# Transposing half of a group's attention probabilities with VectorE and a round trip through DRAM, in eleven of sixteen token tiles

## The chip, the core and the metric

The kernel runs on one core of a Trainium2 chip. The metric is the device time of one execution in microseconds (us). Engines are named as in the profile: PE (TensorE), PEld (its weight loads), DVE (VectorE), ACT (ScalarE), POOL (GpSimd), SP (SyncE, which here only issues DMAs).

## The reference

A transformer block in float32 on 4 sequences of 512 tokens, width 1024, 32 query heads and 8 key heads of 32 columns each:

```python
x = x + layernorm(attention(layernorm(x), w_qkv, b_qkv, w_o, b_o))
x = x + layernorm(lora_moe(layernorm(x), gate_w, base_w, base_b, lora_A, lora_B))

# attention
qkv = x @ w_qkv.T + b_qkv              # then rope on q and k
scores = einsum('bhqd,bhkd->bhqk', q, k) / sqrt(32), causal
attn = softmax(scores)
out = einsum('bhqk,bhkd->bhqd', attn, v) @ w_o.T + b_o
# lora_moe: a dense product x @ base_w.T, plus the two best of 8 rank-16 adapters
```

## The kernel before

The 2048 tokens are 16 tiles of 128 (four per sequence, i = 0 to 3 within it); a list `line` holds them in the order of the work, 0 to 11, 13, 14, 15, 12. Tiles go in pairs through the three big products (q, o and f): `seven` (L655) does a pair with seven products instead of eight, with sums of operands and of weights. Weight pieces of 128x512 (256 KB) come from DRAM into a ring of RING = 13 buffers, each for one product, in the order in which PE uses them (`bring_pieces`, L476). Keys, values and gate use weights that stay in SBUF.

**Attention of a tile** goes in groups (`Group`, L1371). A group has n heads of each of four key heads ("quads" r = 0 to 3), so that a quad's scores fill at most 512 columns: n = 4 for i = 0, 2 for i = 1, 1 for i = 2 and 3. It has m = n(i+1) blocks of 128x128 per quad. There are 88 groups. The steps of one group:

1. `scores` (L1382): PE writes q times k of the four quads, side by side on 32-row tiles of the array, into the one PSUM tile `sc`.
2. Softmax: DVE adds the mask and finds the negated maximum (two quads at a time, L1459 and L1469); ACT takes the exponentials with their sums into `pr` in SBUF (L1411); DVE inverts the sums (L1440); POOL scales `pr` (L1425).
3. `turn` (L1480), once per quad: PE transposes the m blocks of `pr` into PSUM (`pt_p`, L1485); `copy` brings them to SBUF as `prT`.
4. `values` (L1498): PE multiplies `prT` of the four quads, side by side, with v into `av` (L1508), and a copy brings that to `aT`, the input of product o.

`copy` (L331) may go to ACT (L335) or DVE (L336), whichever is free first. It serves `prT`, `aT`, and the turned x, h, k and low-rank tiles.

**What sets the order.** Every engine executes its instructions in the order in which they were issued; waits are semaphores. The order is worked out when the program is built, by a planner (`Order`, L92): operations have costs in us, are put on the engine where they start first, and PE picks the next step from lanes: scores, turns, the value lane (a group's four turns, then its values), and the dense products. `_choice` (L202) prefers what is ready; scores and values that could go together are put directly one behind the other, since both use tiled parts of the array:

```python
        value = values[0] if values and values[0].tiled else None
        waiting = []
        if score is not None and value is not None:
            if self._comes(score):
                waiting.append(values)
            if self._comes(value) and not self._is_ready(value):
                waiting.append(scores)
```

The value lane is filled at L1623: `value_lane += g.turned + [g.valued]`. A group's scores also wait for the turns of the group two before (L1611). `pr` and `prT` of one quad take one 2 KB slot each of SOFT = 8. PSUM has 4 banks (`ps`) besides `sc`. All DMAs are issued by SP, in order; an issue waits there for its buffer, and what stands behind it waits too. The planner counts 2.8 us from the end of a DMA's transfer until it has landed (LANDS) and 370 KB per us (RATE).

Of the kernel before, what the change touches and what calls it, by code (L numbers as in the profile page):

```python
# [11 lines left out]
F32 = mybir.dt.float32  # L12
# [4 lines left out]
P = 128  # L17
# [5 lines left out]
MASKED = -1e30  # L23
QUADS = P // HD


# [4 lines left out]
FILL = 0.3  # L31
# [60 lines left out]
class Order:  # L92
# [109 lines left out]
    def _choice(self, scores, values, lanes):  # L202
# [7 lines left out]
        if score is not None and value is not None:  # L210
            if self._comes(score):
                waiting.append(values)
            if self._comes(value) and not self._is_ready(value):
                waiting.append(scores)
        for lane in lanes:
# [20 lines left out]
    def tensor(self, scores, urgent, values, dense):  # L236


        while True:
# [17 lines left out]
            for step in steps:  # L257
                self._take(step)
            self.now += us
            for step in steps:  # L260
                step.done.finish(self.now + FILL)
        self.run(float("inf"))
# [3 lines left out]
def kernel(  # L266
# [26 lines left out]
    QSCALE = 1.0 / math.sqrt(HD)  # L293
    BANKS, SOFT, RING = 4, 8, 13

# [35 lines left out]
    def copy(n, out, in_):  # L331

        return Op(
            0,
            act=(0.15 + n * 0.00085, lambda: nc.scalar.copy(out(), in_())),  # L335
            dve=(0.15 + n * 0.00105, lambda: nc.vector.tensor_copy(out(), in_())),  # L336
        )
# [507 lines left out]
    for n, tok in enumerate(line):  # L845
        tok.before = line[n - 1] if n else None
        tok.last = n == T - 1
    pairs = [line[n : n + 2] for n in range(0, T, 2)]

    def load_x(job):  # L850
# [520 lines left out]
    class Group:  # L1371
        def __init__(self, tok, at, n):
            self.tok, self.seq, self.at, self.n = tok, tok.seq, at, n
            self.kt = at // GROUP
            self.name = f"{tok.t}_{at}"
            self.parts = 2
            self.exps, self.normed = [Task() for _ in range(QUADS)], [Task() for _ in range(QUADS)]
            self.rtot = [Task() for _ in range(QUADS // 2)]
            self.pr, self.prT = [None] * QUADS, [None] * QUADS
            self.has_prT = [Task() for _ in range(QUADS)]  # L1380

    def scores(g):  # L1382
# [19 lines left out]
        def quadrant(r):  # L1402
            urgent = 1 + r / QUADS
            yield soft_slots.take()
            pr = soft.tile([P, GROUP, P], F32, tag="soft", name=f"pr_{g.name}_{r}")
            pr = g.pr[r] = pr.rearrange("p a b -> p (a b)")
            for c in range(g.n):
                yield act(
                    0.5 + n * 0.00079,
                    urgent,  # L1410
                    lambda: nc.scalar.activation(  # L1411
                        pr[:, c * n : (c + 1) * n],
                        sc4[:, r, c, :],
                        AF.Exp,
                        bias=nmax[:, r, c : c + 1],
                        accum_out=total[:, r, c : c + 1],
                    ),
                )
            g.exps[r].finish(order.at)
            yield g.rtot[r // 2]  # L1420
            for c in range(g.n):
                yield pool(
                    0.33 + n * 0.00089,
                    urgent,
                    lambda: nc.gpsimd.tensor_scalar(  # L1425
                        pr[:, c * n : (c + 1) * n],
                        pr[:, c * n : (c + 1) * n],
                        rtot[:, r, c : c + 1],
                        1.0,
                        ALU.mult,  # L1430
                        ALU.mult,
                    ),
                )
# [10 lines left out]
        def softmax():  # L1444
# [8 lines left out]
            for r0 in range(0, QUADS, q):  # L1453
# [19 lines left out]
                for r in range(r0, r0 + q):  # L1473
                    start(quadrant(r), order.at)

        start(softmax(), order.now)
        for h in range(QUADS // 2):
            start(totals(h), order.now)

    def turn(g, r):  # L1480

        m = g.n * (g.tok.i + 1)
        pt = ps.tile([P, 4, P], F32, tag="ps", name=f"pt_p_{g.name}_{r}")
        for j in range(m):
            nc.tensor.transpose(pt[:, j, :], g.pr[r][:, j * P : (j + 1) * P], ident)  # L1485

        def end():
            yield g.turned[r].done
            soft_slots.give(order.at)
            yield soft_slots.take()  # L1490
            prT = g.prT[r] = soft.tile([P, NQ, P], F32, tag="soft", name=f"prT_{g.name}_{r}")
            yield copy(m * P, lambda: prT[:, :m, :], lambda: pt[:, :m, :])
# [5 lines left out]
    def values(g):  # L1498

        tok, i = g.tok, g.tok.i  # L1500
        if tok.aT is None:
            tok.aT = acts.tile([P, ND, P], F32, tag="aT", bufs=3, name=f"aT_{tok.t}")
        av = ps.tile([P, GROUP, P], F32, tag="ps", name=f"av_{g.name}")
        for c in range(g.n):
            for j in range(i + 1):
                for r in range(QUADS):
# [3 lines left out]
                        lhsT=g.seq.v[j][:, head * HD : (head + 1) * HD],  # L1510
                        rhs=g.prT[r][:, c * (i + 1) + j, :],
                        start=(j == 0),
# [3 lines left out]
        def end():  # L1516
            yield g.valued.done
            for r in range(QUADS):
                soft_slots.give(order.at)
# [86 lines left out]
    for k, g in enumerate(groups):  # L1606
# [4 lines left out]
        if k > 1:  # L1611
# [4 lines left out]
            Step(0.109 * blocks, partial(turn, g, r), [g.normed[r | 1]], bank=True, turns=True)  # L1616
            for r in range(QUADS)
        ]
# [3 lines left out]
        score_lane.append(g.scored)  # L1622
        value_lane += g.turned + [g.valued]  # L1623

# [129 lines left out]
```

## Time and profile before

| | |
|---|---|
| three runs, us | 1163.79, 1162.33, 1164.63; median 1163.79 |
| the profiled execution, us | 1164.45, its span 1162.7 |
| granted PE clock | 0.996 |
| instructions in the span | 21371 |
| HBM read, written | 209.09 MB, 20.97 MB: 198 GB/s over the span |
| pieces issued | 664 of 256 KB |
| pt_p transposes | 1280 (320 for each of the four quads) |

The span is the time between the first and the last instruction of the profile; the execution's time has 1.75 us around it. Busy times of an engine overlap with those of others, so they do not add up. A PE matmul's duration is longer than its spacing to the next one, since matmuls are pipelined; what PE spends is read from where the next one begins. One float32 product is two instructions, a transpose one. In the groups of the profile, "out<-in" names the tiles, x the count, then come busy us, mean ns of one, and the idle time before them with what ended it.

### The profile page before, as it was taken

Reading aid. Unit: us, or ns where it says so; the run is one execution under the profiler, and the core shown is the slowest. Engines: PE = TensorE matmul, PEld = TensorE weight load, DVE = VectorE, ACT = ScalarE, POOL = GpSimd, SP = SyncE. Lnnn points to the kernel's source line nnn. Section 1 sums busy time; section 2 is a strip of 40 time slices with the busy share of each in tenths; the row PEclk is TensorE's granted clock in tenths of the full one; section 3 lists DMA queues with packets and bytes.
Section 4 is the critical chain, followed back from the end, with each engine's and each line's share of the span. In section 5 each row is a group of like instructions: output and inputs, shape, how many; then the busy total and the mean of one; then the engine's idle time right before and its main releaser. Section 6 shows DMA issues by size and latency. Waiting matters only on the chain.

```text
span 1162.7 us, 21371 instructions
## 1 busy us (share of the span) xinstructions
PE 1136.4 (98%) x7240; PEld 624.5 (54%) x7240; DVE 832.6 (72%) x1629; ACT 530.1 (46%) x1545; POOL 611.7 (53%) x859
## 2 busy tenths in 40 slices
PE   7999999999999999999999999999999999999997
PEld 3455554655556455565555555456555555556443
DVE  4787767987678756787667876768866787668564
ACT  0354554555555355555434434455644555454010
POOL 2686856743756435544555253654545564547231
PEclk9999999999999999999999999999999999999999
DMA  9879777563773637625477443673457745585783
GB/s 349 277 255 310 248 253 263 170 220 97 257 239 96 199 109 253 192 83 176 141 244 256 137 135 118 219 229 106 149 168 233 243 135 160 164 268 187 221 285 118
DMA packets 117740, 231.48 MB, mean 199 GB/s; under 512 B 13440, under 2 KB 14464, under 8 KB 117632
## 3 DMA queue, kind: packets, MB, share of 16 engines
q1 hardware_dynamic: 117632, 230.12, 60.7%
q8 instruction: 58, 0.95, 0.3%
q14 instruction: 50, 0.41, 0.1%
HBM read 209.09 MB, written 20.97 MB: 198 GB/s over the span
## 4 chain that ended last, share of the span: by engine, by line
PE 86%; DVE 7%; DMA 3%; POOL 1%; ACT 1%; issue 1%; SPq 0%; POOLq 0%; ACTq 0%
PE acc_f L618 18%; PE acc_o L618 16%; PE acc_q L618 14%; PE pt_p L1485 11%; PE acc_kv L618 8%; PE sc L1390 7%; PE av L1508 6%; PE acc_gl L618 2%; DVE nmax L1469 2%; PE pt_xn L593 1%; PE pt_h L593 1%; DMA piece<-in_w_qkv_dram 1%; ACT pr L1411 1%; PE pt_q L1010 1%; DMA xa<-in_x_dram 1%
## 5 line engine op out<-in xcount | busy, mean ns | idle before, releaser
L1425 POOL TENSOR_SCALAR pr<-pr,rtot 128x256 f32<-128x256 f32 (+3 forms) x512 | 300.5, 602 | 251.9 <-DVE rtot L1440 183.3
L1411 ACT ACTIVATE pr<-sc,nmax 128x256 f32<-128x256 f32 (+3 forms) x512 | 265.0, 536 | 121.8 <-DVE nmax L1469 63.6
L1469 DVE TENSOR_REDUCE nmax<-sc 128x2 f32<-128x768 f32 (+3 forms) x176 | 198.2, 1126 | 33.7 <-ACT pr L1411 30.6
L1485 PEld LDWEIGHTS pt_p<-ident,pr 128*128 128x128 f32 x1280 | 144.5, 141 | 59.3 <-issue 49.1
L1485 PE MATMUL pt_p<-ident,pr 128*128 128x128 f32 x1280 | 173.2, 276 | 2.4 <-DVE raw_q L727 1.0
L335 ACT COPY prT<-pt_p 128x512 f32<-128x512 f32 (+1 forms) x261 | 134.1, 548 | 62.4 <-PE pt_p L1485 61.0
L1459 DVE TENSOR_TENSOR sc<-sc,cmask 128x256 f32<-128x256 f32 (+2 forms) x176 | 96.7, 550 | 48.6 <-PE sc L1390 39.0
L335 ACT COPY aT<-av 128x128 f32<-128x128 f32 (+2 forms) x83 | 26.1, 315 | 222.1 <-PE av L1508 222.0
L618 PE MATMUL acc_f<-piece,s_f 128*128 128x512 f32 x256 | 120.1, 602 | 2.1 <-DVE s_f L343 2.1
L618 PE MATMUL acc_kv<-wkv_sb,T_xn 128*128 128x512 f32 x256 | 119.4, 597 | 0.0
L1411 ACT ACTIVATION_READ_ACCUMULATOR pr<-sc,nmax 128x1 f32 x512 | 108.3, 212 | 0.0
L618 PE MATMUL acc_o<-piece,aT 128*128 128x512 f32 x232 | 105.9, 594 | 0.0
L618 PE MATMUL acc_q<-piece,s_q 128*128 128x512 f32 x224 | 105.4, 595 | 0.1
L618 PE MATMUL acc_q<-piece,T_xn 128*128 128x512 f32 x224 | 103.9, 594 | 0.1
L618 PE MATMUL acc_o<-piece,s_o 128*128 128x512 f32 x224 | 102.8, 593 | 0.0
L1390 PE MATMUL sc<-kT,qT 32*128 32x384 f32 (+3 forms) x1024 | 93.9, 464 | 0.5 <-ACT pr L1411 0.5
L1508 PEld LDWEIGHTS av<-prT,v 128*32 128x32 f32 x2560 | 64.8, 109 | 50.1 <-issue 35.0
L618 PE MATMUL acc_f<-piece,T_h 128*128 128x512 f32 x192 | 90.0, 592 | 0.0
L343 POOL TENSOR_TENSOR y<-y,w 128x512 f32<-128x512 f32 x61 | 79.1, 1309 | 20.3 <-ACT w L568 14.9
L1508 PE MATMUL av<-prT,v 128*32 128x128 f32 x2560 | 88.7, 276 | 0.2 <-DVE prT L336 0.2
L336 DVE COPY prT<-pt_p 128x512 f32<-128x512 f32 (+1 forms) x91 | 58.3, 642 | 31.3 <-PE pt_p L1485 29.7
L541 POOL TENSOR_TENSOR rstd<-veps,neg_half 128x1 f32<-128x1 f32 x64 | 35.0, 549 | 86.1 <-DVE veps L537 85.8
(154 smaller groups left out, 1416.3 us busy)
## 6 DMA issues: line engine op xcount, KB each, us to landing
piece<-mixed_f SPq DMA_DIRECT2D x128, 256.0 KB, 3.5
piece<-in_w_o_dram SPq DMA_DIRECT2D x116, 256.0 KB, 3.6
piece<-mixed_q SPq DMA_DIRECT2D x112, 256.0 KB, 3.4
piece<-mixed_o SPq DMA_DIRECT2D x112, 256.0 KB, 4.1
piece<-in_w_qkv_dram SPq DMA_DIRECT2D x100, 256.0 KB, 3.7
piece<-in_w_base_dram SPq DMA_DIRECT2D x96, 256.0 KB, 3.3
xa<-in_x_dram SPq DMA_DIRECT2D x32, 256.0 KB, 3.8
y<-in_x_dram SPq DMA_DIRECT2D x16, 512.0 KB, 5.7
```

The source lines that it names most:

```text
L335: act=(0.15 + n * 0.00085, lambda: nc.scalar.copy(out(), in_())),
L336: dve=(0.15 + n * 0.00105, lambda: nc.vector.tensor_copy(out(), in_())),
L343: engine.tensor_tensor(out=out(), in0=in0(), in1=in1(), op=op)
L541: nc.gpsimd.tensor_tensor(out=self.rstd, in0=self.veps, in1=neg_half, op=ALU.pow)
L618: nc.tensor.matmul(acc[0][:, :n], lhsT=lhsT(c), rhs=w(c), start=(c == 0), stop=last)
L1390: nc.tensor.matmul(sc[:, r, c * n : (c + 1) * n], lhsT=tok.qT[g.kt][rows, (g.at + c) % GROUP, :], rhs=seq.kT[g.kt][rows, :n], start=True, ...
L1411: lambda: nc.scalar.activation(pr[:, c * n : (c + 1) * n], sc4[:, r, c, :], AF.Exp, bias=nmax[:, r, c : c + 1], accum_out=total[:, r, c : ...
L1425: lambda: nc.gpsimd.tensor_scalar(pr[:, c * n : (c + 1) * n], pr[:, c * n : (c + 1) * n], rtot[:, r, c : c + 1], 1.0, ALU.mult, ALU.mult,),
L1459: lambda: nc.vector.tensor_tensor(out=diag, in0=diag, in1=cmask.unsqueeze(1).unsqueeze(1).to_broadcast([P, q, g.n, P]), op=ALU.add,),
L1469: lambda: nc.vector.tensor_reduce(nmax[:, some, : g.n], sc4[:, some], AX.X, ALU.max, negate=True),
L1485: nc.tensor.transpose(pt[:, j, :], g.pr[r][:, j * P : (j + 1) * P], ident)
L1508: nc.tensor.matmul(av[r * HD : (r + 1) * HD, c, :], lhsT=g.seq.v[j][:, head * HD : (head + 1) * HD], rhs=g.prT[r][:, c * (i + 1) + j, :], ...
```

## The change

In the eleven tiles `line[3:14]` (3 to 11, 13 and 14), quads 2 and 3 of every group are no longer turned by PE. There are 64 such groups: 24 with four blocks per quad of tiles with i = 3, 4 of i = 0 and 12 of i = 1 (also four blocks), and 24 of i = 2 with three blocks. For them:

- `pr` of a pair of quads is one tile, and for quads 2 and 3 its columns are laid out as (strip s of 32 keys, quad, block, key in strip), so ACT and POOL write runs of 32 floats.
- `flip`: DVE transposes the 32x32 blocks in place (one instruction of 128 x 2m·128), SP writes the tile to DRAM (`there`), waits until it has landed, and reads it back with four DMAs, one for each strip of keys, into `flat`, in runs of 2m·32 floats.
- `values` reads its moving operand for those quads as four strips of 32 columns.

Everywhere: a group's values stand behind the next group's turns in the value lane; `pr` and `prT` are kept by pairs of quads (SOFT = 6 slots of 4 KB instead of 8 of 2 KB); RING goes from 13 to 9; `copy` goes to ACT alone; `_choice` no longer holds scores back for values; and the planner takes the scores of a scores-and-values pair as done before the values.

```diff
-            if self._comes(value) and not self._is_ready(value):
-                waiting.append(scores)
...
+            first = self.now + (us if len(steps) == 1 else steps[0].us + TILING / 2)
             self.now += us
-            for step in steps:
-                step.done.finish(self.now + FILL)
+            for step, at in zip(steps, (first, self.now)):
+                step.done.finish(at + FILL)
...
-    BANKS, SOFT, RING = 4, 8, 13
+    BANKS, SOFT, RING = 4, 6, 9
+    FROM, TO = 3, 14
+    SIDE = 32
+    NS = P // SIDE
...
             act=(0.15 + n * 0.00085, lambda: nc.scalar.copy(out(), in_())),
-            dve=(0.15 + n * 0.00105, lambda: nc.vector.tensor_copy(out(), in_())),
...
+    flipped = line[FROM:TO]
...
+            self.by_tensor = QUADS // 2 if tok in flipped else QUADS
...
+            if r < g.by_tensor:
+                pr = g.pr[r // 2][:, r % 2]
+                to = [pr[:, c * n : (c + 1) * n] for c in range(g.n)]
+                exp_in = [sc4[:, r, c, :] for c in range(g.n)]
+                exp_out = to
+            else:
+                j = tok.i + 1
+                strips = g.pr[r // 2][:, :, r % 2]
+                to = [strips[:, :, c * j : (c + 1) * j, :] for c in range(g.n)]
+                exp_in = [
+                    sc4[:, r, c, :].rearrange("p (j s k) -> p j s k", s=NS, k=SIDE)
+                    for c in range(g.n)
+                ]
+                exp_out = [a.rearrange("p s j k -> p j s k") for a in to]
...
+    def flip(g):
+        m = g.n * (g.tok.i + 1)
+        h = g.by_tensor // 2
+        yield g.normed[g.by_tensor :]
+        pr = g.pr[h].rearrange("p s r m k -> p (s r m k)")
+        yield dve(
+            0.1 + 2 * m * P * 0.00105,
+            1,
+            lambda: nc.vector.transpose(out=pr, in_=pr),
+        )
+        there = dram.tile(
+            [NS, SIDE, NS, 2 * m * SIDE], F32, tag="there", bufs=4, name=f"there_{g.name}"
+        )
+        yield sp(
+            P * 2 * m * P * 4 / 1024 / RATE,
+            lambda: nc.sync.dma_start(out=there.rearrange("a k s r -> (a k) (s r)"), in_=pr),
+            -1,
+        )
+        yield LANDS
+        soft_slots.give(order.at)
+        yield soft_slots.take()
+        flat = g.prT[h] = g.new("flat", h)
+        def read():
+            for s in range(NS):
+                nc.sync.dma_start(
+                    out=flat[s * SIDE : (s + 1) * SIDE].rearrange("p a r m q -> p a (r m q)"),
+                    in_=there[:, :, s, :].rearrange("a k r -> k a r"),
+                )
+        yield sp(NS * 0.37, read, -1)
+        yield LANDS
+        for r in range(g.by_tensor, QUADS):
+            g.has_prT[r].finish(order.at)
...
+        def rhs(r, m):
+            prT = g.prT[r // 2]
+            if r < g.by_tensor:
+                return prT[:, r % 2, m * P : (m + 1) * P]
+            return prT[:, :, r % 2, m, :]
...
-                        rhs=g.prT[r][:, c * (i + 1) + j, :],
+                        rhs=rhs(r, c * (i + 1) + j),
...
-            for r in range(QUADS)
+            for r in range(g.by_tensor)
...
-        value_lane += g.turned + [g.valued]
+        value_lane += g.turned + ([groups[k - 1].valued] if k else [])
+    value_lane.append(groups[-1].valued)
```

In the issue order of the changed program SP has 64 writes to `there` and 256 reads of `flat` more.

## The prediction

> **What bounds the kernel now.** I read the busy table first, then the chain of work that ended last, then the groups, the waits and the DMA issues.
>
> ```profile
> PE 1136.4 (98%) x7240; PEld 624.5 (54%) x7240; DVE 832.6 (72%) x1629; ACT 530.1 (46%) x1545; POOL 611.7 (53%) x859
> ...
> PE 86%; DVE 7%; DMA 3%; POOL 1%; ACT 1%; issue 1%; SPq 0%; POOLq 0%; ACTq 0%
> ...
> L1485 PE MATMUL pt_p<-ident,pr 128*128 128x128 f32 x1280 | 173.2, 276 | 2.4 <-DVE raw_q L727 1.0
> L335 ACT COPY prT<-pt_p 128x512 f32<-128x512 f32 (+1 forms) x261 | 134.1, 548 | 62.4 <-PE pt_p L1485 61.0
> ...
> L336 DVE COPY prT<-pt_p 128x512 f32<-128x512 f32 (+1 forms) x91 | 58.3, 642 | 31.3 <-PE pt_p L1485 29.7
> ...
> q1 hardware_dynamic: 117632, 230.12, 60.7%
> ```
>
> PE is busy for 98% of the span and 86% of the chain is PE; the DMA queues' packets fill 60.7% of 16 engines. A PE instruction that goes away shortens the end, if nothing else holds PE up. The 276 ns on the transposes (the turns) is a latency, since matmuls overlap; the spacing comes from the chain in order of time (start, length, what):
>
> ```profile
> 92.24 1.31 PE pt_p L1485 x12
> ...
> 304.16 10.30 PE acc_o L618 x24
> ```
>
> A turn occupies PE for 1.31/12 = 0.109 us, and a 512-wide product (two instructions) for 2 x 10.30/24 = 0.858 us. In the timeline a group's scores of 512 columns take 1.07 us (750.68 to 751.75), its values 1.01 us (756.24 to 757.25). PE is idle for only 1162.7 - 1136.4 = 26 us, most of it at both ends, so time can come only from PE's own work.
>
> **What is removed.** In the issue order of the changed program PE has 816 pt_p transposes instead of 1280; all other PE counts are equal. 464 x 0.109 = **50.6 us off PE**. The 128 copies of those turns go (40 quad pairs of 512 columns, 24 of 384). All remaining PSUM copies are on ACT. By the rows (587 ns for 512 columns, 482 for 384, 266 to 372 for smaller ones), ACT's copies go from 183.7 to 202.4 us, so ACT stands at about 549 us of busy time; DVE loses 91.1 us of copies. A copy can now stand behind an exponential (0.69 + 0.21 us) where DVE used to take it. At the 58 copies of x, h, k and the low-rank tile that went to DVE, that is at most 52 us; at best nothing. I take nothing, since PE's waits for copies were 0.7 us (turns on ACT's prT) and 0.2 (values on DVE's): dense products lie between, and they stay.
>
> **What is added.** Sixty-four DVE block transposes, 40 of 128x1024 and 24 of 128x768. No such row exists. The nearest are DVE's reductions over the same sizes, 1223 and 957 ns: 40 x 1.223 + 24 x 0.957 = 71.9 us. DVE ends at 832.6 - 91.1 + 71.9 = 813 us, still under PE. Half price would be 36 us less, double 72 us more, which is 885 us and still hidden as busy time; only its 1 to 2.4 us in each group's own path counts.
>
> DMA: 464 blocks of 64 KB are 30.4 MB written and 30.4 MB read. 292 MB over some 1130 us is 258 GB/s. These 10 us stretches show what the queues carried:
>
> ```profile
> 10.00:20.00 10.00, 10.00 (x24) 4.45 (x23) 3.98 (x11) 0.00 (x0) 1.37 (x2) 1.00 1.07 378
> 20.00:30.00 10.00, 9.93 (x31) 4.63 (x30) 4.79 (x9) 0.59 (x1) 4.07 (x5) 1.00 1.05 393
> ```
>
> (The last column is GB/s.) So the mean fits; peaks may not.
>
> SP: 64 writes and 256 reads, 320 x 0.33 to 0.38 us = 106 to 122 us of issue on a queue that mostly waits for free piece buffers:
>
> ```profile
> SPq L489 <- PE acc_q L618: 231.7, 167, 20.6
> SPq L489 <- PE acc_f L618: 224.2, 184, 10.9
> ```
>
> Strided access: the softmax of the moved quads writes runs of 32 floats, and PE reads the values' moving operand in such runs. For POOL there is a row: the rotary product with a 32-wide broadcast (L780) takes 1321 ns, the plain addition of equal size 1309, so I count nothing. For ACT and PE none exists. DVE's 16-wide runs (565 ns for 256 elements, against 429 for the mask addition of 256) are a third dearer; on ACT that would be some 0.2 us per exponential, hidden by an engine idle half the time. For the values the bounds are nothing and double time, 232 blocks x 0.218 = 50.6 us (a group of four blocks takes 1.01, of which about 0.14 is the entry). I take nothing, since turns and products run at one column rate whatever the operand (0.109 for 128 columns, 0.429 for 512), and keep the upper end.
>
> Order: the before order has 74 values directly after scores, the changed one 57. The timeline shows about 0.09 us at entering tiled work (products of 3.44 us fill 3.53 before the scores at 763.44). 17 x 0.09 = **1.5 us**.
>
> **The new wait: values for the round trip.** A moved group's values wait for scores, softmax, block transpose, write, landing, four reads, landing. Behind the values on PE everything waits, since its order is fixed. From the timeline, scores' end to the last normalised quad takes (medians) 10.0 us for tiles of three key blocks, 10.8 for four, 13.8 for two, 18.9 for one. To this comes T: DVE 1.2, plus 0.4 for its queue; the write; four read issues, 1.3; the last landing. DMA landings:
>
> ```profile
> DMA to landing us min/median/max: 2.6/5.8/8.8
> ```
>
> is for the 512 KB stores of mixed weights. The 256 KB loads of x:
>
> ```profile
> DMA to landing us min/median/max: 2.7/3.8/6.6
> ```
>
> Middle: 1.6 + 5.8 + 1.3 + 3.8 = 12.5. Ends: 1.6 + 2.6 + 1.3 + 2.7 = 8.2 and 1.6 + 8.8 + 1.3 + 6.6 = 18.3.
>
> Against this stands the PE work that the order puts between a group's scores and its values. Laid end to end at the spacings above it is 21.6 to 38 us in tiles of three and four blocks (half of them under 26.5), 25.5 and more for two, 30.9 and more for one. Walking the 64 groups, each shortfall pushing all that follows, the stalls sum to: T = 11: 0; 12: 2; 13: 7; 14: 15; 16: 39; 18: 70 us. T = 12.5 gives 4; landings scatter, so I take **6 us**.
>
> **Fewer piece buffers, 13 to 9.** Along the orders, the PE work between the release of a buffer and the use of its next piece is at least 10.3 us before and 6.9 after; 85 of 655 have under 8. Piece landings are 3.1 to 4.3 us. But SP stands at a read until its write has landed: typically four pieces lie between, 3.4 us of PE work, against 5.8 for the landing. That is 2.4 us of waiting and 1.3 of issuing with pieces behind it, so the next piece is some 2.8 us late and needs 2.8 + 4 = 6.8, or 7.8 with a 5 us landing. Ends: nothing, and 1 us at half of the 64 groups, 32 us. I take **10 us**, a third of a microsecond at half of them.
>
> **Sum**, against the profiled execution's 1164.45 us (span 1162.7; the median of the runs is 1163.79, 0.1% lower): 1164.45 - 50.6 + 1.5 + 6 + 10 = **1131 us**.
>
> The Trainium skill speaks against the route. "VectorE: DVE Perf Modes", in "The three transpose paths", warns that a plain DMA copy with strides for a transpose is 19 times slower than the hardware's own when the innermost destination stride is large. No row of before shows such a copy; here DVE turns the 32x32 blocks and the reads keep runs of 768 or 1024 bytes, so the condition isn't met. If it held all the same, 30.4 MB at a nineteenth of 378 GB/s would alone take some 1500 us, an estimate by that page. "DMA: Bandwidth & Descriptors", "Anatomy of one DMA", gives about 2.0 us plus bytes over 436 GB/s on its other path: an estimate of 3.2 us for each way, T about 8, no late values and 1125 us. The trace's 5.8 us stores are dearer, and I go by them.
>
> **Rivals.**
> 1. *All is hidden.* For: the order leaves 21.6 us and more. Against: before's stores under load. 1164.45 - 50.6 + 1.5 = 1115.
> 2. *Pieces starve.* Nine buffers and a third more DMA traffic, above all in stretches of seven-product work with groups between, where about 7 pieces and 1 MB of round trip fall in some 8.7 us: 2.9 MB, 330 GB/s. For: landings there would be nearer to the first 160 us (6.0 us for pieces of w_qkv). Against: 378 GB/s was carried. The upper end, 32 us, with the 6: about 1153.
> 3. *The round trip is too long: slower.* Place: the values' wait for the four reads. If T is 16 or more, by small packets of 1 KB or by SP standing behind a piece, stalls of 39 us and 10 for pieces eat the 49; at T = 17 (54 us) with 10 it is 1179. The turning point is T = 16. For: the largest landings, 8.8 and 6.6. Against: medians stay at 12.5.
> 4. *The strided operand makes values dearer.* At the upper end 50.6 us: the gain is gone and with the 16 of stalls it ends at 1182; at half of that, 1156.
>
> **Chances.** Forecast (1116 to 1145) 0.45; all hidden 0.10; pieces 0.19, of which 0.02 within 0.2%; round trip 0.18; strips 0.08, of which 0.03 faster, 0.02 same, 0.03 slower. Faster by over 0.2% (what a measurement of this kernel can tell): 0.45 + 0.10 + 0.17 + 0.03 = 0.75; within: 0.04; slower: 0.21. The range 1110 to 1172 leaves out the dearest part of rivals 3 and 4, under 0.2. The forecast's sign holds most of the chance.
>
> **What would show it.** Right: 816 transposes at the same spacing; values waiting for the flat reads for under 10 us in all; PE 97% busy or more; DVE transposes near 1.2 us; stores landing in 5 to 6 us, reads in about 4. Wrong: LDWEIGHTS of the values waiting on a DMA for tens of us (rival 3); products waiting for pieces for over 20 us (rival 2); values of 1.01 us growing to 1.5 or more (rival 4). A DVE transpose of over 2.5 us, or exponentials a third dearer, would also break the sum, since every group's path lengthens with them.

## The result and the profile after

The changed kernel takes 1193.56 us (median of four runs, 1193.10 to 1194.06), the kernel before beside it 1163.13 (four runs): a ratio of 1.026, 95% interval 1.0242 to 1.0278. The change makes the kernel 30 us slower; 1131 us was forecast, and the range ended at 1172. The profiled execution took 1193.11 us, its span 1191.4, at a mean granted PE clock of 0.984 (before 0.996).

The page of the changed kernel, in its own order: busy times, the main DMA queue, the chain by engine, three groups, the issues of the round trip.

```profile
PE 1111.7 (93%) x6776; PEld 582.7 (49%) x6776; DVE 807.9 (68%) x1533; ACT 535.5 (45%) x1573; POOL 616.2 (52%) x863
...
q1 hardware_dynamic: 163712, 290.95, 76.8%
...
PE 47%; DMA 17%; DVE 3%; SPq 2%; POOL 1%; ACT 1%; issue 1%; POOLq 0%; ACTq 0%; DVEq 0%
...
L339 ACT COPY prT<-pt_p 128x512 f32<-128x512 f32 (+1 forms) x224 | 111.7, 552 | 64.6 <-PE pt_p L1566 53.8
L621 PE MATMUL acc_o<-piece,s_o 128*128 128x512 f32 x224 | 108.8, 616 | 22.6 <-DMA piece<-in_w_o_dram 14.1
...
L1566 PE MATMUL pt_p<-ident,pr 128*128 128x128 f32 x816 | 115.5, 281 | 9.3 <-DVE raw_q L730 4.2
...
there<-pr SPq DMA_DIRECT2D x40, 512.0 KB, 4.7
flat<-there SPq DMA_DIRECT2D x160, 128.0 KB, 4.6
```

The 464 turns are gone (x816), yet PE is idle for 1191.4 - 1111.7 = 79.7 us, 53 more than before, and DMA holds 17% of the span in the chain where it held 3% (the chain could be followed over 72% of the span only). The turns that are left keep their spacing (in the chains, where the clock is full, 16 of them take 1.76 to 1.90 us before and 1.90 after), so 464 x 0.109 = 50.6 us of PE's work were gained. The span grew by 28.7 us all the same: some 79 us were lost elsewhere, 53 of them as idle time of PE. The waits of PE and of its weight loads (us in total, times, longest), then those of SP's queue:

```profile
PEld acc_o L621 <- DMA piece<-in_w_o_dram: 20.3, 10, 4.4
PE acc_o L621 <- DMA piece<-in_w_o_dram: 14.1, 10, 3.5
PE av L1602 <- DMA flat<-there: 10.5, 7, 4.2
```

```profile
SPq L492 <- PE acc_q L621: 123.9, 103, 12.4
SPq L492 <- PE acc_f L621: 116.2, 143, 16.9
SPq L1549 <- DMA there<-pr: 103.4, 59, 5.3
```

All products together wait 23.8 us on PE for pieces, the values 10.5 for `flat`; in the kernel before PE has neither wait (only its weight loads wait for pieces, 15.5 us, here 45.7). SP stands at 59 reads until their store has landed, 103 us in all. One such place in the timeline (start, length, engine, line; in brackets the idle time before, with what ended it):

```profile
254.82 0.36 SPq L1539 DMA_DIRECT2D there<-pr  x1
255.30 1.29 SPq L872 DMA_DIRECT2D xa<-in_x_dram  x2
...
261.89 0.41 PE L1602 MATMUL av<-prT,v 128*32 128x128 f32 x4
261.93 1.75 SPq L1549 DMA_DIRECT2D flat<-there  x4
...
266.47 0.43 PE L1602 MATMUL av<-flat,v 128*32 128x128 f32 x2 [4.17 <-DMA flat<-there]
...
266.66 0.46 PE L1602 MATMUL av<-flat,v 128*32 128x128 f32 x2
...
266.87 0.46 PE L1602 MATMUL av<-flat,v 128*32 128x128 f32 x2
```

The store is issued at 254.82, the reads only 7.1 us later, the values run at 266.47: 11.65 us from the store's issue, and PE stands for 4.17. Then look at the last rows: the entries come every 0.21 us, where other values come every 0.11. The table of 2 us stretches says why (busy us of PE, PEld, DVE, ACT, POOL, each with its count; then the granted clock, the DMA share, GB/s):

```profile
262.00:264.00 2.00, 0.30 (x4) 0.03 (x3) 1.94 (x2) 0.77 (x3) 1.84 (x3) 1.00 0.42 125
264.00:266.00 2.00, 0.00 (x0) 0.00 (x0) 1.96 (x4) 0.68 (x3) 2.00 (x2) 0.87 0.98 290
266.00:268.00 2.00, 1.53 (x28) 1.50 (x28) 0.29 (x1) 0.00 (x0) 2.00 (x3) 0.50 0.94 383
268.00:270.00 2.00, 2.00 (x9) 1.25 (x6) 0.00 (x0) 0.79 (x3) 0.06 (x1) 0.50 0.81 169
270.00:272.00 2.00, 2.00 (x4) 0.88 (x3) 1.23 (x3) 0.74 (x3) 0.96 (x2) 0.50 0.83 280
272.00:274.00 2.00, 2.00 (x13) 0.70 (x12) 0.39 (x2) 0.59 (x1) 0.83 (x1) 0.92 0.23 84
```

After some 4 us without work the granted clock is 0.50 for 6 us. By an estimate from these rows, a stall of 4 us thus costs about 3 us more, in which PE is "busy". The Trainium skill, "TensorE: Matmul & The Clock Gate", Part 1, says the same: half the clock after an idle window of about 3.4 us, full clock after a busy one. Not every stall of that length shows it here: after one of 3.53 us, which ends at 629.13, the next two stretches of 2 us are at 1.00, and 0.53 comes only behind a further stall of 2.20 us.

A second place shows a stall of another kind, right behind a short wait for `flat`:

```profile
319.63 0.39 PE L1602 MATMUL av<-flat,v 128*32 128x128 f32 x4
...
320.06 0.59 ACT L339 COPY aT<-av 128x512 f32<-128x512 f32 x1 [2.03 <-PE av L1602]
...
324.89 0.66 DVE L346 TENSOR_TENSOR s_o<-s_o,aT 128x512 f32<-128x512 f32 x1
...
325.69 2.04 PE L621 MATMUL acc_o<-piece,s_o 128*128 128x512 f32 x2 [5.68 <-ACT pr L1442]
```

These values (1.3 us late) are the last of their pair. Product o needs their `aT` and its sum `s_o`, which DVE executes only at 324.89, behind masks and maxima of the next groups, which themselves wait for exponentials on ACT. PE has no other work in its order there, so it stands for 5.68 us more. (The releaser named, an exponential, isn't what the product reads; `s_o` is.) It is tempting to put this stall down to the late values, but it isn't theirs: in **a_values** and **a_tiny** below no value waits for the round trip on PE, and the stall is there all the same, 5.65 us long. It belongs to the order in which the planner put the work. Two more are like it: 4.16 us before the turns at 980.17 and 5.27 us before those at 1078.16. a_tiny has all three:

```profile
314.60 5.46 PE L621 MATMUL acc_o<-piece,s_o 128*128 128x512 f32 x6 [5.65 <-ACT pr L1442]
...
931.57 1.09 PE L1571 MATMUL pt_p<-ident,pr 128*128 128x128 f32 x4 [4.24 <-DVE raw_q L730]
...
1030.20 2.12 PE L596 MATMUL pt_h<-ident,w 128*128 128x128 f32 x8 [5.27 <-DVE w L565]
```

They are 15.1 of the changed kernel's 79.7 us of idle time. After its start the kernel before has no stall longer than 2.1 us.

### The profile page after: what moved, and what is told of

Same layout as the page of the kernel before. It is cut to its first block, busy times and chain, and to the rows that moved or that the text cites. A ratio compares the mean times of both kernels' runs of the same rounds, so it can differ in the third digit from the quotient of the medians.

```text
span 1191.4 us, 20840 instructions
## 1 busy us (share of the span) xinstructions
PE 1111.7 (93%) x6776; PEld 582.7 (49%) x6776; DVE 807.9 (68%) x1533; ACT 535.5 (45%) x1573; POOL 616.2 (52%) x863
## 3 DMA queue, kind: packets, MB, share of 16 engines
q1 hardware_dynamic: 163712, 290.95, 76.8%
## 4 chain that ended last, share of the span: by engine, by line
PE 47%; DMA 17%; DVE 3%; SPq 2%; POOL 1%; ACT 1%; issue 1%; POOLq 0%; ACTq 0%; DVEq 0%
PE acc_f L621 13%; PE acc_o L621 8%; PE acc_q L621 6%; DMA there<-pr 5%; DMA flat<-there 4%; PE sc L1408 4%; PE acc_kv L621 4%; PE pt_p L1566 4%; PE av L1602 3%; PE acc_gl L621 2%; DMA piece<-in_w_o_dram 1%; DMA out_dram<-y 1%; DMA piece<-mixed_q 1%; SPq L1549 1%; DVE nmax L1500 1%
## 5 line engine op out<-in xcount | busy, mean ns | idle before, releaser
L1490 DVE TENSOR_TENSOR sc<-sc,cmask 128x256 f32<-128x256 f32 (+2 forms) x176 | 97.1, 551 | 68.9 <-PE sc L1408 61.8
L339 ACT COPY prT<-pt_p 128x512 f32<-128x512 f32 (+1 forms) x224 | 111.7, 552 | 64.6 <-PE pt_p L1566 53.8
L621 PE MATMUL acc_o<-piece,s_o 128*128 128x512 f32 x224 | 108.8, 616 | 22.6 <-DMA piece<-in_w_o_dram 14.1
L1566 PE MATMUL pt_p<-ident,pr 128*128 128x128 f32 x816 | 115.5, 281 | 9.3 <-DVE raw_q L730 4.2
L621 PE MATMUL acc_kv<-wkv_sb,T_xn 128*128 128x512 f32 x256 | 122.6, 613 | 0.0
L1566 PEld LDWEIGHTS pt_p<-ident,pr 128*128 128x128 f32 x816 | 92.6, 143 | 48.2 <-issue 35.0
L621 PE MATMUL acc_q<-piece,T_xn 128*128 128x512 f32 x224 | 106.3, 600 | 3.0 <-DMA piece<-in_w_qkv_dram 3.0
L1602 PE MATMUL av<-prT,v 128*32 128x128 f32 x1632 | 91.1, 281 | 0.5 <-DVE w L730 0.3
L1602 PEld LDWEIGHTS av<-prT,v 128*32 128x32 f32 x1632 | 64.2, 111 | 51.2 <-issue 37.2
L621 PEld LDWEIGHTS acc_o<-piece,s_o 128*128 128x128 f32 x224 | 40.4, 193 | 70.1 <-issue 34.8
```

Of the source, the lines that this page charges most:

```text
L621: nc.tensor.matmul(acc[0][:, :n], lhsT=lhsT(c), rhs=w(c), start=(c == 0), stop=last)
L1490: lambda: nc.vector.tensor_tensor(out=diag, in0=diag, in1=cmask.unsqueeze(1).unsqueeze(1).to_broadcast([P, q, g.n, P]), op=ALU.add,),
L1566: nc.tensor.transpose(pt[:, j, :], pr[:, j * P : (j + 1) * P], ident)
L1602: nc.tensor.matmul(av[r * HD : (r + 1) * HD, c, :], lhsT=g.seq.v[j][:, head * HD : (head + 1) * HD], rhs=rhs(r, c * (i + 1) + j), start=(j ...
```

## The experiments

Each kernel is compared with the kernel before in runs on the same chip; "+8" means 8 us above that. The kernel before itself varied from 1163.1 to 1164.1 between the calls, and the changed kernel is at +30.4.

### Waits and traffic of the round trip

**a_values** lets the values of quads 2 and 3 read strips of `prT` of quads 0 and 1; order, instructions and DMAs stay. The computation leaves out the probabilities of the moved quads.

```diff
-            return prT[:, :, r % 2, m, :]
+            n = g.n * (i + 1) * P
+            near = g.prT[0][:, r % 2, :n].rearrange("p (s m q) -> p s m q", s=NS, q=SIDE)
+            return near[:, :, m, :]
```

> The changed kernel, but the values of quads 2 and 3 read strips of prT of quads 0 and 1, so PE never waits for the round trip; every DMA, its waits and the issue order of all engines stay (attention's result is another one). Theory V (PE stands at the values until the reads have landed, and that makes up the loss): at most 1150. Theory S (SP stands at the stores until the block transposes are done and at the reads until the stores have landed, and weight pieces behind it come late): 1175 to 1190, only the 17 us that PE and its weight loads wait for the reads can go. Theory O (the new order, nine buffers and copies on ACT alone cost it): 1180 to 1193.

**a_sp_free** keeps the values' wait, but stores from weights in SBUF and reads from an input (`fixed`, a view of `w_base` of the same shape), so that SP waits neither for DVE nor for a landing. What the moved quads use is not the transposed probabilities.

```diff
-                in_=there[:, :, s, :].rearrange("a k r -> k a r"),
+                in_=fixed[:, :, s, :].rearrange("a k r -> k a r"),
...
-            lambda: nc.sync.dma_start(out=there.rearrange("a k s r -> (a k) (s r)"), in_=pr),
+            lambda: nc.sync.dma_start(out=there.rearrange("a k s r -> (a k) (s r)"),
+                in_=wkv_sb[:, :2, :].rearrange("p c e -> p (c e)")[:, : 2 * m * P]),
```

> The changed kernel, but the stores take their data from a constant tile and the reads theirs from a weight matrix, in the same shapes: SP waits neither for the block transposes nor for the stores' landing; traffic, issue order and the values' wait for the reads stay (the values get other data). Theory S: at most 1155, with PE's waits for pieces gone. Theory V: about 1165, since the reads also start 4 to 6 us earlier. Theory W (the 61 MB of traffic slow the pieces by themselves): above 1180. Theory O: above 1180.

**a_traffic_only** has both edits: the same 60 MB in the same places, and nobody waits for the round trip.

> Both edits together: no value waits for a read, SP never waits for a round trip, only the traffic and its 320 issues stay (other data again). Theories S and V: 1120 to 1140, the time forecast with little stall. Theory W: above 1160. Theory O: above 1160.

**a_stores_only** is a_traffic_only with the reads cut to 32-byte runs (32 a read); **a_tiny** cuts the stores too (128 runs of 32 bytes a store). The number of DMAs stays.

```diff
-                    out=flat[s * SIDE : (s + 1) * SIDE].rearrange("p a r m q -> p a (r m q)"),
-                    in_=fixed[:, :, s, :].rearrange("a k r -> k a r"),
+                    out=flat[s * SIDE : (s + 1) * SIDE].rearrange("p a r m q -> p a (r m q)")[:, 0, :8],
+                    in_=fixed[0, :, s, :8],
```

> As a_tiny, but the stores carry their full 30 MB in runs of 3 and 4 KB; only the reads in runs of 768 and 1024 bytes are cut. If the bytes count alike, half way between a_tiny and a_traffic_only (1174). If the short runs of the reads are what loads the queues: within 5 us of a_tiny. If stores are dearer: within 5 us of 1174.

> The changed kernel with no wait of values or of SP on the round trip (as in a_traffic_only), and stores and reads cut to 32 bytes a run, so that the issues, the order and the nine buffers stay and the 61 MB are gone; attention's result is another one. Theory W (the bytes themselves slow the weight pieces): 1130 to 1140, that is the time without the round trip (1182) less 51 us of turns. Theory O2 (the order, which was planned around landings, holds PE up even with no traffic): 1160 to 1175, as with the traffic. Theory I (the 320 issues on SP): 1160 to 1175 as well, with SP busy at L1549.

| kernel | median us | against before | PE idle | DMA queue time |
|---|---|---|---|---|
| changed | 1193.56 | +30.4 | 79.7 | 76.8% |
| a_values | 1175.51 | +11.4 | 69.9 | 76.9% |
| a_sp_free | 1179.86 | +15.7 | 68.9 | 77.8% |
| a_traffic_only | 1173.69 | +9.6 | 66.0 | 78.9% |
| a_stores_only | 1149.60 | -13.8 | 49.8 | 67.8% |
| a_tiny | 1148.30 | -15.1 | 47.8 | 61.2% |

Taking away either wait alone gives 19.0 or 14.7 us, both together 20.8: the two do not add. Without the values' wait PE still waits 21.2 us for pieces; without SP's standing (12 of its 103 us are left) it waits 12.0 for pieces and 11.0 for `flat`; without both it is 19.0 for pieces. No run shows why the gains overlap. So neither Theory S nor Theory V alone holds (a_values lies in S's range, but a_sp_free is 25 us above it), and a_traffic_only is where W and O put it. a_tiny lies between the ranges of its theories: without the bytes it is faster than before, but not by all of the turns.

Then the traffic: stores of 30 MB cost 1.3 us, which the scatter of the runs can't tell from nothing, reads of the same 30 MB 23.4 (PE is idle for 16.2 us more, and waits 15.8 more for pieces). a_stores_only is within 5 us of a_tiny, as expected if the short runs of the reads are what loads the queues. Queue time (share x 16 engines x span) is 11198 engine-us in a_tiny, 12437 with the stores, 14768 with the reads: 1239 for the stores, whose runs are 3 or 4 KB, and 2331 for the reads, whose runs are 768 or 1024 bytes. Each figure is what the whole queue's time grows by, so whatever other packets lose beside the new ones is in it. a_traffic_only in stretches of 20 us (columns as above), and its longest waits for pieces:

```profile
460.00:480.00 20.00, 18.85 (x127) 9.16 (x126) 14.11 (x23) 9.38 (x25) 10.99 (x14) 1.00 1.05 338
480.00:500.00 20.00, 17.21 (x119) 7.99 (x118) 14.06 (x25) 8.51 (x23) 9.76 (x13) 1.00 1.08 296
```

```profile
PEld acc_o L621 <- DMA piece<-in_w_o_dram: 14.5, 10, 5.0
PEld acc_o L621 <- DMA piece<-mixed_o: 11.4, 17, 2.3
PE acc_o L621 <- DMA piece<-in_w_o_dram: 8.0, 6, 4.2
```

The queues are full (1.05, 1.08) at 296 to 338 GB/s, where the first stretches of the kernel before carried 378 and 393. Pieces land in 4.1 to 5.1 us (medians by kind; 3.3 to 3.8 in a_tiny), and PE waits for them for 19.0 us in all (1.7 in a_tiny).

**a_long_reads** turns the layout in DRAM round: four stores of 32 partitions write the short runs, and one read takes 3 or 4 KB per partition.

```diff
+                    out=there[:, :, a, :].rearrange("s k r -> k s r"),
+                    in_=pr[a * SIDE : (a + 1) * SIDE].rearrange("k (s r) -> k s r", s=NS),
...
+                out=flat.rearrange("p a r m q -> p (a r m q)"),
+                in_=there.rearrange("s k a r -> (s k) (a r)"),
```

> The changed kernel with another layout of the tile in DRAM: it is written by four DMAs of 32 partitions in runs of 768 or 1024 bytes and read back by one DMA whose partitions each take one run of 3 or 4 KB. Same bytes, same number of DMAs (five a group). Theory 1 (it is reads in short runs that load the queues: 2331 engine-us for 30 MB against 1239 for the stores of long runs): queue share from 77% to 71 or 72%, time 1165 to 1178. Theory 2 (short runs cost the same in either direction): queue share 76 to 78%, time 1188 to 1198. Theory 3 (short runs cost more where they are written): queue share over 79%, over 1200 us.

1187.05 us (+23.2, interval of the ratio 1.0194 to 1.0237), queue share 74.4%: between the theories. Queue time falls by 14640 - 14088 = 552 engine-us, half of the 1092 by which reads were dearer than stores. Short runs are dear in both directions, more so where they are read; that it is the reads alone is refuted. The 7 us of time aren't the layout's alone: the planner is given another duration for the read, and in the order that it makes the stalls of 4.16 and 5.27 us are shorter (2.18 and 1.86).

### The ring, the slots and the lane

**noflip** sets `FROM, TO = 0, 0`: all 1280 turns on PE, no round trip, all else of the change. **noflip_dve_copies** is noflip where DVE may take copies again. **before_ring9** is the kernel before with `RING = 9`. **noflip_old_lane** is noflip with the lane, the choice and the done time of before:

```diff
-        value_lane += g.turned + ([groups[k - 1].valued] if k else [])
-    value_lane.append(groups[-1].valued)
+        value_lane += g.turned + [g.valued]
...
+            if self._comes(value) and not self._is_ready(value):
+                waiting.append(scores)
...
-            for step, at in zip(steps, (first, self.now)):
+            for step, at in zip(steps, (self.now, self.now)):
```

> The changed kernel with no tile sent by way of DRAM (an empty range of tiles): all turns on PE, but values behind the next group's turns, nine piece buffers, pairs of quads and copies on ACT stay. Theory O: 1190 or more, since 50 us of turns come back and its losses stay. Theories S, V and W: 1160 to 1175.

> The kernel before with nine piece buffers instead of thirteen, nothing else. If the smaller ring costs the 18 us that the change costs without a round trip: 1176 to 1185. If not: 1163 to 1168.

> The changed kernel with all turns on PE (1182 in the last runs), and copies again on ACT or DVE, whichever is free. If copies on ACT alone cost the 18 us against before: 1164 to 1168. If it is the values' later place or the nine buffers: 1176 to 1185.

> The changed kernel with no quad flipped (all 1280 turns on PE), and with the value lane, the choice between scores and values and the done time of a pair as in the kernel before; what is left of the change is the ring of nine, slots by pairs of quads and copies on ACT alone. Known: the same without these three (noflip) 1182.4 us, the kernel before with a ring of nine 1177.9, the kernel before 1163.4. Theory 1 (a group's values behind the next group's turns costs at the end of the attention, where noflip loses about 12 us between 1040 and 1080 us): 1171 to 1178 and no such loss there. Theory 2 (the ring of nine, and slots that are held by pairs, cost whatever the lane): 1180 to 1186.

| kernel | median us | against before | interval of the ratio |
|---|---|---|---|
| noflip | 1182.43 | +18.3 | 1.0133 to 1.0166 |
| noflip_dve_copies | 1189.65 | +26.3 | 1.0199 to 1.0244 |
| before_ring9 | 1177.90 | +14.5 | 1.0099 to 1.0146 |
| noflip_old_lane | 1168.40 | +4.6 | 1.0028 to 1.0059 |

noflip lies between the ranges of its theories, noflip_dve_copies above both of its own, and before_ring9 where a costly ring puts it. Theory 1 of the last holds, with a time a little under its range: without flips the new lane (with the choice and done time, undone together) costs 13.7 us. Ring of nine, slots by pairs and copies on ACT alone together cost only 4.6. A ring of nine in the kernel before costs 14.5 though, and with only 1.6 us of PE's waits for pieces, so late pieces aren't its price; that it is the order which the planner makes with nine buffers is an inference. In noflip ACT alone is not a cost: with DVE back it is 8 us slower. Where the lane's time goes, noflip first, then noflip_old_lane, and the wait in noflip:

```profile
1060.00:1080.00 20.00, 13.97 (x130) 12.21 (x131) 10.62 (x34) 8.79 (x22) 11.28 (x25) 0.74 0.07 26
```

```profile
1060.00:1080.00 20.00, 19.73 (x121) 12.12 (x120) 12.57 (x30) 10.97 (x38) 12.12 (x24) 1.00 0.61 196
```

```profile
1064.37 1.08 PE L596 MATMUL pt_h<-ident,w 128*128 128x128 f32 x4 [5.27 <-DVE rtot L1471]
```

At the end of the attention dense products have run out (26 GB/s of pieces), PE stands for 5.27 us for the normalised h, and the clock falls to 0.74 in the mean; with the old lane products are left there.

**flip_old_lane** makes the same three edits in the changed kernel.

> The changed kernel with the flips, but with the value lane, the choice and the done time of the kernel before: a group's values stand behind its own turns, so they wait in the lane for the round trip and the next group's turns wait behind them. Theory 1 (this order costs whatever is flipped: without flips the old order was 14 us faster, 1168.4 against 1182.4): 1175 to 1183. Theory 2 (with flips the later place of the values is what hides the round trip, so the old order loses more than it gains): over 1195, with values waiting for flat, or PE idle while dense work runs out, for 30 us and more.

1235.77 us (+72.1): theory 2. With flips the old lane is 42 us dearer than the new one. With these flips the new lane can't simply be given back.

```profile
PE av L1604 <- DMA flat<-there: 40.3, 16, 10.0
```

**a_soft5** has `BANKS, SOFT, RING = 4, 5, 11`.

> The changed kernel with five slots of 4 KB for probabilities instead of six and eleven piece buffers instead of nine. Theory 1 (pieces come too late because there are few buffers: PE and its weight loads wait for pieces for some 34 us in the changed kernel): these waits fall to under 20 us, time 1178 to 1186. Theory 2 (the slots bind at least as much): PE waits for the softmax and the turns in their place, over 1193 us.

1227.89 us (+64.0): theory 2. PE's waits for pieces fell from 23.8 to 11.0 us, but the reads of the round trip now wait for a slot that earlier values still hold:

```profile
SPq L1549 <- PE av L1602: 30.0, 16, 5.6
```

In the changed kernel this row has 6.1 us. In this planner's order a slot is worth more than two piece buffers. (Not all of the loss is that wait: PE also stands for 7.3 and 6.8 us before low-rank turns, for DVE's gate.)

### The planner's landing

**a_lands** counts 4.8 us for a landing instead of 2.8, in `flip` alone. The edit changes only when the planner believes that the tiles arrive, but with that the order of what it plans behind them. The planner's landing counts from the end of a transfer, at 370 KB per us: with 2.8 a store of 512 KB lands 4.2 us after its issue (measured 4.7 in the median), the four reads 4.3 us after the first issue (measured, 1.3 to the last issue and 4.6 from there, about 5.9). So the 4.3 us of the expectation, which count from the issue, are not to be set against 2.8.

```diff
-        yield LANDS
+        yield LANDS + 2
         soft_slots.give(order.at)
...
         yield sp(NS * 0.37, read, -1)
-        yield LANDS
+        yield LANDS + 2
```

> The changed kernel with the planner's landing time raised from 2.8 to 4.8 us for the store and for the reads of the round trip, so that it places the reads and the values later. The landings measured were 4.3 us in the median. Theory 1 (the 20 us of the waits are the planner's: it issues values and reads too early): waits of values for flat fall from 12.9 us to under 3, SP's standing on the store from 103 to under 60, time 1173 to 1182. Theory 2 (the waits come from queues that are full, or other work has to fill the added time and there is none): 1188 to 1200.

1171.56 us (+7.7; five runs, 1163.46 to 1178.88, a wide scatter): 22 us off the changed kernel, a little more than theory 1 expected, though not by the waits it named first. Those of PE and SP in it:

```profile
PE av L1602 <- DMA flat<-there: 5.0, 6, 1.6
```

```profile
SPq L1549 <- DMA there<-pr: 58.5, 31, 5.5
```

The values' wait on PE halved (10.5 to 5.0), but with their weight loads it is 9.8 us of 12.9, where under 3 was expected; SP stands 45 us less at its reads, as expected, PE is idle for 63.7 us instead of 79.7, and with fewer long stalls the clock is 0.991 instead of 0.984. But two of the stalls that aren't due to the round trip, of 5.68 and 4.16 us, are gone as well, while the third has grown from 5.27 to 7.76. So how much of the 22 us is the later landing and how much an order that happens to be better is not shown.

Last, combinations. **lands_lane**: 4.8 us and a mixed lane (own turns for groups without flips, and the old choice and done time). **lands3_lane**: the same with 5.8. **lands_long_lane**: lands_lane with the layout of a_long_reads. **lands_long** and **lands3_long**: the changed kernel's own lane, that layout, and 4.8 or 5.8 us. (In the expectation of lands3_lane "millisecond" should read microsecond.)

```diff
-        value_lane += g.turned + ([groups[k - 1].valued] if k else [])
-    value_lane.append(groups[-1].valued)
+        last = groups[k - 1] if k else None
+        value_lane += g.turned + ([last.valued] if last and last.by_tensor < QUADS else [])
+        value_lane += [g.valued] if g.by_tensor == QUADS else []
+    value_lane += [groups[-1].valued] if groups[-1].by_tensor < QUADS else []
```

> The changed kernel with the planner's landing at 4.8 us for both legs of the round trip, the old choice and done time, and a lane in which the values of a group without flips stand behind its own turns and those of a group with flips behind the next group's turns. Theory 1 (the planner's wrong landing and the lane are two separate losses, 22 and up to 14 us, of which the part at the end of the attention and in the tiles without flips comes back): 1158 to 1166. Theory 2 (the later landing has already taken what the lane could give): 1168 to 1175.

> As the kernel with landings of 4.8 us and the mixed lane, and the tile in DRAM laid out so that the reads take runs of 3 or 4 KB in one DMA (the stores, four DMAs, take the short runs). Alone the layout gave 6.5 us and took the queue share from 76.8 to 74.4%. Theory 1 (queue load still costs): 6 us or more under the kernel without the layout, 1152 to 1160. Theory 2 (with the values late enough the queues' load no longer shows): within 3 us of it.

> As the kernel with landings of 4.8 us and the mixed lane, with 5.8 us. A dose test of the planner's landing. Theory 1 (2.8 was too small against 4.3 in the median and 7.4 at most, and a millisecond more only costs slots): the waits of values for flat shrink further, time within 4 us of the kernel with 4.8. Theory 2 (the time hangs on the chance order that the planner makes, not on the landing): it differs by over 6 us in either direction, with other waits than those for flat.

> The changed kernel with its own lane, the planner's landing at 4.8 us for both legs, and the layout in DRAM that is read in runs of 3 or 4 KB. Theory 1 (the landing took 22 us off, and the layout 12 us where the landing was right): 1157 to 1166, so about the kernel before (1163.6). Theory 2 (the two take away the same waits): 1167 to 1174.

> The same with 5.8 us. Under the mixed lane 5.8 was 11 us faster than 4.8. Theory 1 (a landing that is nearer to the slowest reads keeps helping): 1150 to 1160, under the kernel before by 0.3% or more. Theory 2 (that gain was one of order, not of the landing): within 6 us of the kernel with 4.8, in either direction.

| kernel | median us | against before | interval of the ratio | PE idle |
|---|---|---|---|---|
| lands_lane | 1182.66 | +19.0 | 1.0153 to 1.0195 | 68.8 |
| lands_long_lane | 1170.76 | +7.1 | 1.0045 to 1.0075 | 65.6 |
| lands3_lane | 1171.88 | +8.2 | 1.0051 to 1.0090 | 64.2 |
| lands_long | 1168.99 | +5.2 | 1.0038 to 1.0074 | 60.9 |
| lands3_long | 1166.35 | +2.6 | 1.0011 to 1.0043 | 64.1 |

The mixed lane (with the old choice and done time) gives nothing: 11 us dearer than a_lands, above both of its theories. A landing of 5.8 us is 11 us faster than 4.8 under it, but PE waits for `flat` in neither (its weight loads 6.4 and 2.6 us): theory 2 of lands3_lane, another order. In the changed kernel's own lane the step is worth 2.6 us, and the runs of the two overlap: theory 2 of lands3_long. The layout gives 12 us under the mixed lane, as theory 1 of lands_long_lane had it, though 1170.8 lies above its 1152 to 1160; in the own lane it gives 2.5, theory 2 of lands_long. No version that computes the whole result beats the kernel before. In the best one (the profile is of its slowest run, 1171.97 us) PE's list has no wait for `flat` any more, and pieces are the largest wait, 17.1 us on PE:

```profile
PEld acc_o L621 <- DMA piece<-mixed_o: 22.5, 21, 4.2
...
PE acc_o L621 <- DMA piece<-mixed_o: 12.0, 12, 3.4
```

## Why the prediction was wrong, point by point

The distances to the kernel before make a ledger: 4.6 for ring, slots and copies (noflip_old_lane); 13.7 for the lane (to noflip); -50.6 for the turns; 17.2 between that sum, -32.3, and a_tiny's -15.1; 1.3 for the stores' traffic; 23.4 for the reads'; 20.8 for the waits. They add to 30.4 by construction; since the terms overlap (the layout and the landing above), each is the price in its place in this sequence, not a cost of its own.

1. **The turns, 50.6 us: right.** 464 are gone, and those that are left keep their spacing.
2. **DVE's block transposes, 1.22 and 0.96 us: right.**

```profile
L1531 DVE STREAM_TRANSPOSE pr<-pr 128x1024 f32<-128x1024 f32 x40 | 49.4, 1234 | 1.9 <-POOL pr L1456 1.9
...
L1531 DVE STREAM_TRANSPOSE pr<-pr 128x768 f32<-128x768 f32 x24 | 23.3, 969 | 0.2 <-POOL pr L1456 0.2
```

3. **Strided access at nothing: right.** The values of a group of four blocks still take 1.01 us when half of them come from `flat` (257.28 to 258.29; the prediction's sign against it was 1.5); one takes 280 ns from `flat` and 281 from `prT`; exponentials of 512 columns 692 ns (687 before). Rival 4 falls.
4. **Copies on ACT at nothing: right, as far as noflip tells** (with DVE back it is slower).
5. **"So the mean fits": failed.** The round trip's traffic was put at nothing, because bytes were compared with GB/s that pieces had shown. But a byte of the reads adds 2331/1239 = 1.9 times the queue time of a byte of the stores, and the queues fill at 296 to 338 GB/s. That is 23.4 us, by late pieces: rival 2, and for another reason than it gave. Its line of over 20 us of products waiting was passed (23.8). The Trainium skill, "DMA: Bandwidth & Descriptors", "Specifications", puts the size from which the full rate is had at 512 bytes; the runs here were 768 and 1024 bytes and didn't have it, so the measurement decides.
6. **The values' wait, 6 us: the round trip was right, its price was not.** With medians of 4.7 and 4.6 us, T is 1.6 + 4.7 + 1.8 + 4.6 = 12.7 for groups of four blocks (12.5 was taken). The walk gave 4 us at that T; PE waited 10.5 us for `flat`, and the waits, with SP's standing, cost 20.8. It used one T for all groups, where landings of 2.3 to 7.0 and 1.9 to 7.4 us were seen, and it priced a stall at its length, where the one of 4.17 us is followed by half the clock. Rival 3 said that T must be 16 for the kernel to be slower; by the medians T stayed under 13. (The "T about 8" of the estimate beside the sum leaves out the 1.3 us of issuing; 9.3 gives no late values either.)
7. **"Order: 1.5 us": the step that failed most.** Counting entries to tiled work left out that another order can leave PE without work: where dense products run out the later values cost 13.7 us without any flip, and most of the 17.2 of point 9 is of the same kind.
8. **Nine buffers, 10 us: too dear, as far as it can be told.** Ring, slots and copies cost 4.6 together without the round trip; SP's standing is part of the 20.8. Nine buffers may also have a share in the 23.4 of the reads, since fewer buffers leave less time for a late piece (with eleven PE waited 11.0 us for pieces, in a slower kernel); the reads were not run with thirteen.
9. **The 17.2 us of a_tiny: for the most part order, as far as the traces tell.** It has the changed order, the same number of DMAs, and next to no traffic. Against noflip PE is idle for 10.2 us more (47.8 and 37.6), and by the mean clocks, 0.988 and 0.993, some 5 us more of clock are lost. Of the three stalls shown with the profile, 5.65, 4.24 and 5.27 us, noflip has only the last, which is part of the 13.7. The other two, 9.9 us, are about the idle time that came on top, and half the clock follows each. No DMA is what they wait for: PE stands for DVE's results with nothing else ready in its order. No run takes them away alone.

Rivals 2 and 3 were counted as alternatives. They came together, with the cost of the order, which neither named.

## What to carry to other kernels

Work that is taken off the busiest engine pays only if what replaces it fits the queues by their busy time, not by bytes; find the price of the new run length first. Price a wait on a fixed-order engine with the loss of clock after it. Before a stall is put down to the wait just ahead of it, look for the same stall in a run without that wait: here the one of 5.68 us stayed. And where a planner sets the order, price the new order by itself, by running it without the work that it was made for (noflip, a_tiny): here, by the ledger, it cost more than the traffic did. One constant of the planner moved the time by 22 us, and two further buffers bought at the price of one slot lost 33.6.

## What the runs showed of the hardware

- Adding 30 MB of DMA reads from DRAM in runs of 768 to 1024 bytes added 1.9 times the queue time that 30 MB of stores in runs of 3 to 4 KB had added (2331 against 1239 engine-us). With the short runs on the stores' side both legs add 2890 together, against 3442 in the changed kernel.
- PE's granted clock was 0.50 for about 6 us after a stall of 4.17 us, and 1.00 after one of 3.53 us. By an estimate from the means, 0.996 before and 0.984 after, (1 - 0.984) x 1191.4 = 19 us of clock were lost, against 4.7.
- A DVE transpose of 32x32 blocks over 128x1024 float32 took 1234 ns, about as long as a DVE maximum over as many elements (1223 ns).
